# Relational pass of a graph network with FFN: epilogue and FFN of a node range as two chains, one range apart, spread over the gathers

## The chip, the cores and the metric

The kernel runs on one core of a Trainium2 chip. The metric is the device time of one execution in microseconds (us), as the median of several. The engines are TensorE (PE in the profile, its weight loads PEld), VectorE (DVE), ScalarE (ACT), GpSimd (POOL) and SyncE (SP). SP and POOL issue the DMAs of the part that is looked at here: SP plain loads and stores, POOL gathers of rows by a list of indices.

## The reference, cut to what matters

The input is a graph of 12,500 nodes with 256 features and 212,500 edges, which are sorted by their destination. Two layers follow one another, each a graph part and an FFN part. The change lies in the first layer:

```
x = x + L0_gnn(layernorm(x))        # per edge: weight * (x[src] @ block-diagonal W[relation]), summed at dst
x = x + L0_ffn(layernorm(x))        # rows picked by a router (top-k): gelu(xn @ w1 + b1) @ w2 + b2, times the router's weight
x = x + L1_gnn(layernorm(x))        # attention over the same edges
x = x + L1_ffn(layernorm(x))        # two of eight experts per row
```

The FFN of the first layer has 1024 hidden columns. This kernel computes it for all nodes, and weighs or drops it later, when the router's choice among all nodes is known.

## The kernel before, in words

The kernel has these stages, with their place in the profile. From 0 to 465 us it computes a table T0 in device memory: for each of 8 relations the products of all normalized nodes with that relation's block-diagonal matrix. From 465 to 2906 us runs the **relational pass** (`even_depths`). Its last chains end at 2979 us. Then come the choice of the router (`choose`, to 3055 us), the combination of FFN and nodes (to 3230 us), the attention pass over the same edges (to 6030 us) and the experts (to 7439 us).

In the relational pass the edges are cut into NT = 1661 tiles of 128. Tile t takes these steps:

- `fetch(t)`: POOL gathers 128 rows of 1 KB from T0 into one of 16 row buffers (L234, `row<-T,rowC`).
- `matrices(j)`: for 6 tiles at a time (SUB) DVE makes matrices `S`, 128 edges by 96 destinations (WIN): one where the edge goes to the destination (L922), times the edge's weight (L1017). There are 4 such buffers.
- `use(t)`: TensorE multiplies the gathered rows with `S` and adds the products in PSUM to the sums of the node range (L913, `bin<-S,row`). A range has 512 nodes (BIN), its sums lie transposed in two banks, and two ranges fit into the pool `psA`. There are 24 ranges of four node tiles and a last one of two. A range has some 68 edge tiles (1661 / 24.4).

The order of the work is written by hand with a small planner, `Plan`: a heap of pieces of work by step. A step is a tile of edges. `fetch(t)` is at step t, `use(t)` at step t + 3, `matrices(j)` at t - 8 of its first tile. The heap is run from its smallest step up, and what it emits fixes the order of instructions on PE, DVE, ACT and SP. POOL has the gathers alone.

When the last tile of a range has been added, the generator `summed(b, sums)` is put in a queue (`plan.queue(line, ...)`). A generator does a piece of work, yields a number of steps, and is continued that many steps later. The queue `line` runs one range's chain after another. Before the change one chain does all for a range, in 59 or 60 steps:

1. The node tiles are loaded (SP), the sums are copied from PSUM (`aT`, L962 on ACT, L963 on DVE).
2. For each of the four node tiles TensorE transposes the sums back (L195, `pt<-ident,aT`), and three steps later DVE adds them to the nodes (L970, `X<-xg,pt`).
3. DVE computes mean and variance of the rows (L201 to L215).
4. For each node tile DVE normalizes (L219, `xn`), one step later TensorE transposes (L195, `pt<-ident,xn`), DVE forms the router's weight (L983) and adds `xn` to `X` (L985), and two steps later the transposed rows are copied to `xT` (L189 on ACT or L191 on DVE, by turns).
5. FFN1: for each of 8 blocks of hidden columns two matmuls (L993, `ph<-xT,w1s`) and gelu on ACT (L995, `hT`), then two steps of distance.
6. FFN2: for each node tile 8 matmuls (L1001, `pt<-w2s,hT`) in two blocks of four, one step apart, then DVE adds b2 (L1007, `y`), and SP stores Y.

So within a range's 68 steps the epilogue (1 to 4) takes the first 31 or so, the FFN the next 28, and the last are free of both. A matmul in this program's 32-bit type leaves two records in the profile. PSUM has eight banks here: four for `psA`, two for `psh` (FFN1), two for `pst`, which the transposes and FFN2 share.

Of the kernel before, what the change touches and what calls it, by code (L numbers as in the profile page):

```python
# [23 lines left out]
F32 = mybir.dt.float32  # L24
# [9 lines left out]
PSUM = bass.MemoryType.PSUM  # L34

P = 128
# [10 lines left out]
SUB = 6  # L47
# [53 lines left out]
def gnn_ffn_kernel(ctx: ExitStack, tc: tile.TileContext, x, src, dst, etype, eweight, w_rel, wr, br,  # L101
                   fw1, fb1, fw2, fb2, W, att_src, att_dst, bias, Wg, bg, W1, b1, W2, b2, out):
    nc = tc.nc
    N, D = x.shape
# [23 lines left out]
    def rows(m):  # L128
        return P if m < NM - 1 else TAIL
# [55 lines left out]
    def evac(dst_ap, src_ap):  # L185

        evac_n[0] += 1
        if evac_n[0] % 2:
            nc.scalar.activation(dst_ap, src_ap, AF.Copy)  # L189
        else:  # L190
            nc.vector.tensor_copy(dst_ap, src_ap)  # L191

    def transpose(o, i):
        k = i.shape[0]
        nc.tensor.transpose(o, i, ident[:k, :k])  # L195
# [14 lines left out]
    def ln_stats(xg, mv, pool):  # L210

        st = pool.tile([P, 4, 6], F32, name="ln_st")
        for i in range(mv.shape[1]):
            nc.vector.bn_stats(st[:, i, :], xg[:, i, :])
            nc.vector.bn_aggr(mv[:, i, :], st[:, i, :])  # L215
        rstd_(mv, pool)

    def normalized(o, xr, mv):
        nc.vector.tensor_scalar(o, xr, mv[:, 0:1], mv[:, 1:2], op0=OP.subtract, op1=OP.mult)  # L219

    def load_nodes(tile_ap, table, ms, eng):

        full = [m for m in ms if rows(m) == P]
        if len(full) < len(ms):
            nc.gpsimd.memset(tile_ap[:, len(full), :], 0.0)
            m = ms[-1]
            eng.dma_start(tile_ap[:TAIL, len(full), :], table[m * P:m * P + TAIL, :])
        if full:
            m = full[0]
            eng.dma_start(tile_ap[:, :len(full), :],  # L230
                          table[m * P:(m + len(full)) * P, :].rearrange("(g p) d -> p g d", p=P))
# [205 lines left out]
    with ExitStack() as ta:  # L437
# [4 lines left out]
        pst = ta.enter_context(tc.tile_pool(name="ta_pt", bufs=2, space=PSUM))  # L442
# [4 lines left out]
        for b in range(NB):  # L447
            k, bl = divmod(b, NB // 2)
            nc.sync.dma_start(BD[bl * SB:(bl + 1) * SB, k, :, bl * SB:(bl + 1) * SB], w4[b])
        T0n = T0.rearrange("(n r) d -> n (r d)", r=R)  # L450
        for ms in GROUPS:
            G = len(ms)
# [4 lines left out]
            for i, m in enumerate(ms):  # L457
                xn = xp_.tile([P, D], F32, name="xn")
                normalized(xn, xg[:, i, :], mv[:, i, :])
                pt = pst.tile([P, 2, P], F32, name="pt")  # L460
                for k in range(2):
                    transpose(pt[:, k, :], xn[:, k * P:(k + 1) * P])
                xT = xp_.tile([P, 2, P], F32, name="xT")
# [11 lines left out]
    KH = FH // P  # L475
# [460 lines left out]
    def even_depths(AD, lcC):  # L936


        with ExitStack() as md:
# [8 lines left out]
            with ExitStack() as r1:  # L948
                wk = r1.enter_context(tc.tile_pool(name="r1_w", bufs=1))
                rw = r1.enter_context(tc.tile_pool(name="r1_r", bufs=16))  # L950
                psA = r1.enter_context(tc.tile_pool(name="r1_pa", bufs=2, space=PSUM))
                psh = r1.enter_context(tc.tile_pool(name="r1_ph", bufs=2, space=PSUM))
                pst = r1.enter_context(tc.tile_pool(name="r1_pt", bufs=2, space=PSUM))
                plan, line = Plan(), []

                def summed(b, sums):
                    ms = [m for m in range(b * BIN // P, (b + 1) * BIN // P) if m < NM]
                    G = len(ms)
                    xg = wk.tile([P, 4, D], F32, name="xg")
                    load_nodes(xg, x, ms, nc.sync)  # L960
                    aT = wk.tile([P, 2, BIN], F32, name="aT")
                    nc.scalar.activation(aT[:, 0, :G * P], sums[0][:, :G * P], AF.Copy)  # L962
                    nc.vector.tensor_copy(aT[:, 1, :G * P], sums[1][:, :G * P])  # L963
                    yield 3
                    for i, m in enumerate(ms):
                        pt = pst.tile([P, 2, P], F32, name="pt")
                        for k in range(2):
                            transpose(pt[:, k, :], aT[:, k, i * P:(i + 1) * P])
                        yield 3
                        nc.vector.tensor_tensor(X[:, m, :], xg[:, i, :], pt.rearrange("p k j -> p (k j)"), op=OP.add)  # L970
                    mv = wk.tile([P, 4, 2], F32, name="mv")
                    ln_stats(X[:, ms[0]:ms[0] + G, :], mv[:, :G], wk)
                    yield 1
                    xT = wk.tile([P, 2, 4 * P], F32, name="xT")
                    for i, m in enumerate(ms):
                        xn = wk.tile([P, D], F32, name="xn", bufs=2)
                        normalized(xn, X[:, m, :], mv[:, i, :])
                        yield 1
                        pt = pst.tile([P, 2, P], F32, name="pt")
                        for k in range(2):  # L980
                            transpose(pt[:, k, :], xn[:, k * P:(k + 1) * P])
                        junk = wk.tile([P, D], F32, name="junk")
                        nc.vector.scalar_tensor_tensor(junk, xn, 1.0, wrB, op0=OP.mult, op1=OP.mult,  # L983
                                                       accum_out=WT[:, m:m + 1])
                        nc.vector.tensor_tensor(X[:, m, :], X[:, m, :], xn, op=OP.add)  # L985
                        yield 2
                        evac(xT[:, :, i * P:(i + 1) * P], pt)
                    yield 2
                    hT = wk.tile([P, KH, 4 * P], F32, name="hT")
                    for f in range(KH):  # L990
                        ph = psh.tile([P, 4 * P], F32, name="ph")
                        for k in range(2):
                            nc.tensor.matmul(ph[:, :G * P], w1s[:, k, f * P:(f + 1) * P], xT[:, k, :G * P],  # L993
                                             start=k == 0, stop=k == 1)
                        nc.scalar.activation(hT[:, f, :G * P], ph[:, :G * P], AF.Gelu_apprx_tanh, bias=b1s[:, f:f + 1])  # L995
                        yield 2
                    yield 1
                    for i, m in enumerate(ms):
                        py = pst.tile([P, D], F32, name="pt")
                        for f in range(KH):  # L1000
                            nc.tensor.matmul(py, hT[:, f, i * P:(i + 1) * P], w2s[:, f, :],  # L1001
                                             start=f == 0, stop=f == KH - 1)
                            if f % 4 == 3:
                                yield 1
                        yield 1
                        y = wk.tile([P, D], F32, name="y", bufs=2)
                        nc.vector.tensor_tensor(y, py, b2B, op=OP.add)  # L1007
                        n = rows(m)
                        nc.sync.dma_start(Y[m * P:m * P + n, :], y[:n])

                add = windows(psA, lambda b, sums: plan.queue(line, plan.now + 1, summed(b, sums)))
                rows_, S_ = {}, {}

                def matrices(j):
                    n = min(SUB, NT - j * SUB)
                    S = one_hot(wk, lcC, j * SUB, n, bufs=4)
                    nc.vector.tensor_tensor(S[:, :n], S[:, :n],  # L1017
                                            ewC[:, j * SUB:j * SUB + n, None].to_broadcast([P, n, WIN]), op=OP.mult)
                    S_[j] = S

                def fetch(t):
                    rows_[t] = rw.tile([P, D], F32, name="row")
                    gather(rows_[t], T0, rowC[:, t:t + 1])

                def use(t):
                    g = rows_.pop(t)
                    add(t, lambda k: g[:, k * P:(k + 1) * P], S_[t // SUB][:, t % SUB, :])

                for t in range(NT):
                    if t % SUB == 0:  # L1030
                        plan.put(t - 8, lambda j=t // SUB: matrices(j))
                    plan.put(t, lambda t=t: fetch(t))
                    plan.put(t + 3, lambda t=t: use(t))
                with tc.manual_schedule(engines=ORDERED):
                    plan.run()
                nc.vector.tensor_scalar(WT, WT, brB, None, op0=OP.add)
            choose(WT)

            with ExitStack() as cb:
                wk = cb.enter_context(tc.tile_pool(name="cb_w", bufs=3))  # L1040
                pst = cb.enter_context(tc.tile_pool(name="cb_pt", bufs=4, space=PSUM))
                psy = cb.enter_context(tc.tile_pool(name="cb_py", bufs=4, space=PSUM))
                for ms in GROUPS:
                    G = len(ms)
# [8 lines left out]
                    for i, m in enumerate(ms):  # L1053
                        n = rows(m)
                        nc.sync.dma_start(X2[m * P:m * P + n, :], X[:n, m, :])
                        xn = wk.tile([P, D], F32, name="xn")
                        normalized(xn, X[:, m, :], mv[:, i, :])
                        pt = pst.tile([P, 2, P], F32, name="pt")
# [621 lines left out]
```

## Time and profile before

| what | value |
|---|---|
| median of 3 executions | 6972.26 us (6971.64 to 6975.37) |
| profiled execution | 7440.8 us, its span 7439.0 us |
| mean TensorE clock in it | 0.719 of full speed |
| relational gathers: first, last start | 464.9 us, 2905.9 us |
| PE, PEld, DVE, ACT, POOL busy over the span | 74%, 62%, 39%, 10%, 55% |

The profiled execution is 6.7% longer than the median. Times of single instructions come from it. A row of the groups reads: line, engine, operation, names of output and inputs, shapes, how often; then busy time in us and the mean ns of one; then the idle time ahead of these instructions and what ended most of it. "issue" is a wait for nothing that the profile shows. The wait's view reads: engine and line that wait, what they wait for, then us in total, times, and the longest.

### The profile page before, as it was taken

The page shows a single profiled execution, that of the slowest core. Times are in us where ns is not written, and L with a number is a line of the kernel's source. Part 1 is how long each engine was busy: PE and PEld are TensorE (multiplying, and loading weights), DVE is VectorE, ACT ScalarE, POOL GpSimd, SP SyncE. Part 2 cuts the span into 40 slices and gives each one's busy share as a digit, 9 for nine tenths or more (in the row PEclk, how much of TensorE's full clock was granted, in tenths as well). Part 3 has the DMA queues.
Part 4 walks back from the last instruction along what each step waited for, and adds up shares of the span by engine and source line. Part 5 has one row for each costly group of instructions (what it writes and reads, how often), then busy time and mean ns, then how long its engine had stood idle before and what let it go on. Part 6 is the DMA issues. An engine that isn't in the chain of part 4 may idle for free. (4 is left out here: it accounts for less than half of the span.)

```text
span 7439.0 us, 75728 instructions
## 1 busy us (share of the span) xinstructions
PE 5498.0 (74%) x26987; PEld 4635.6 (62%) x26987; DVE 2928.5 (39%) x7669; ACT 745.9 (10%) x1537; POOL 4095.7 (55%) x3768
## 2 busy tenths in 40 slices
PE   7967888887788887537777776767867775777775
PEld 3446667666677766427666676766766764666654
DVE  6633222323332222745556565565554650111110
ACT  2310000000000000110000000000000001112111
POOL 0036666666666664047777777777777742222222
PEclk9977787877778888765555555565555557888887
DMA  7753333333333332444444444444444425555555
GB/s 253 300 202 96 102 100 101 100 98 100 101 101 102 102 101 68 150 133 119 123 120 120 124 121 122 124 119 121 122 121 116 126 77 173 138 137 142 137 136 158
DMA packets 437371, 949.39 MB, mean 128 GB/s; under 512 B 84371, under 2 KB 293222, under 8 KB 410783
## 3 DMA queue, kind: packets, MB, share of 16 engines
q0 software_dynamic: 199872, 494.39, 25.6%
q1 hardware_dynamic: 237108, 450.03, 19.4%
q8 instruction: 217, 3.56, 0.2%
q14 instruction: 174, 1.42, 0.1%
HBM read 617.71 MB, written 228.88 MB: 114 GB/s over the span
## 5 line engine op out<-in xcount | busy, mean ns | idle before, releaser
L234 POOL DMA_INDIRECT rows<-T1A,srcC x1661 | 1867.0, 1124 | 684.0 <-issue 455.5
L234 POOL DMA_INDIRECT row<-T,rowC x1661 | 1655.5, 997 | 847.8 <-issue 327.2
L913 PE MATMUL bin<-S,rows 128*128 128x96 f32 (+5 forms) x7700 | 1724.1, 391 | 340.5 <-issue 235.6
L913 PEld LDWEIGHTS bin<-S,rows 128*128 128x128 f32 x7700 | 1604.1, 304 | 444.5 <-issue 315.6
L913 PEld LDWEIGHTS bin<-S,row 128*128 128x128 f32 x7700 | 1232.5, 241 | 237.4 <-issue 221.1
L913 PE MATMUL bin<-S,row 128*128 128x96 f32 (+5 forms) x7700 | 1248.7, 322 | 98.9 <-issue 94.0
L882 POOL DMA_INDIRECT O<-y,toI x210 | 326.7, 1556 | 907.0 <-DVE y L881 419.1
L872 PE MATMUL ph<-xT,we 128*128 128x256 f32 x1680 | 469.7, 442 | 267.7 <-DVE xT L191 262.8
L922 DVE TENSOR_TENSOR S<-lcC,col 128x576 f32<-128x576 f32 x554 | 415.9, 751 | 440.8 <-PE bin L913 175.8
L872 PEld LDWEIGHTS ph<-xT,we 128*128 128x128 f32 x1680 | 372.7, 227 | 344.0 <-DVE xT L191 275.6
L993 PE MATMUL ph<-xT,w1s 128*128 128x512 f32 (+1 forms) x800 | 426.1, 663 | 132.9 <-ACT hT L995 68.6
L1253 DVE TENSOR_TENSOR rows<-rows,w 128x1536 f32<-128x1536 f32 x277 | 484.8, 1750 | 79.6 <-issue 60.9
L861 DVE CAST toI<-xs 128x2 int32<-128x2 f32 x105 | 17.7, 169 | 1024.6 <-DMA O<-y,toI 820.9
L878 PE MATMUL py<-we,hT 128*128 128x256 f32 x1680 | 381.1, 379 | 5.7 <-DVE y L881 5.7
L1001 PE MATMUL pt<-w2s,hT 128*128 128x256 f32 x1568 | 378.5, 385 | 3.2 <-issue 3.1
L469 PE MATMUL pm<-BD,xT 128*128 128x512 f32 x784 | 351.1, 601 | 12.8 <-ACT xT L189 12.3
L878 PEld LDWEIGHTS py<-we,hT 128*128 128x128 f32 x1680 | 318.8, 190 | 50.9 <-DVE y L881 7.7
L195 PE MATMUL pt<-ident,xn 128*128 128x128 f32 x588 | 121.7, 317 | 289.1 <-DVE xn L219 176.0
L993 PEld LDWEIGHTS ph<-xT,w1s 128*128 128x128 f32 x800 | 153.9, 213 | 254.6 <-issue 180.4
L1001 PEld LDWEIGHTS pt<-w2s,hT 128*128 128x128 f32 x1568 | 284.7, 191 | 36.1 <-issue 4.5
L189 ACT ACTIVATE xT<-pt 128x256 f32<-128x256 f32 x301 | 115.2, 383 | 1840.2 <-PE pt L195 979.6
L195 PEld LDWEIGHTS pt<-ident,xn 128*128 128x128 f32 x588 | 79.9, 164 | 342.1 <-issue 317.2
(267 smaller groups left out, 4893.5 us busy)
## 6 DMA issues: line engine op xcount, KB each, us to landing
we<-Wall SPq DMA_DIRECT2D x105, 1026.0 KB
T<-tb SPq DMA_DIRECT2D x97, 1024.0 KB
dmB<-DMN SPq DMA_DIRECT2D x277, 192.0 KB
xs<-XS SPq DMA_DIRECT2D x105, 257.0 KB
row<-T,rowC POOLq DMA_INDIRECT x1661
rows<-T1A,srcC POOLq DMA_INDIRECT x1661
xg<-in_x_dram SPq DMA_DIRECT2D x48, 512.0 KB
T1A<-t SPq DMA_DIRECT2D x97, 130.0 KB
```

Of the source, the lines that this page charges most:

```text
L189: nc.scalar.activation(dst_ap, src_ap, AF.Copy)
L195: nc.tensor.transpose(o, i, ident[:k, :k])
L234: return nc.gpsimd.indirect_dma_start(out=o, out_offset=None, in_=table, in_offset=bass.IndirectOffsetOnAxis(ap=idx, axis=0))
L469: nc.tensor.matmul(pm, xT[:, k, :], BD[:, k, r4:r4 + 4, :], start=True, stop=True)
L872: nc.tensor.matmul(ph, we[:, k * EH + f * P:k * EH + (f + 1) * P], xT[:, k, :], start=k == 0, stop=k == 1)
L878: nc.tensor.matmul(py, hT[:, f, i * P:(i + 1) * P], we[:, A1 + f * D:A1 + (f + 1) * D], start=f == 0, stop=f == KE - 1)
L882: nc.gpsimd.indirect_dma_start(out=O2, out_offset=bass.IndirectOffsetOnAxis(ap=toI[:, i:i + 1], axis=0), in_=y, in_offset=None, compute_op ...
L913: nc.tensor.matmul(open_[b][k][:, lo - b * BIN:hi - b * BIN], lhs(k), S[:, lo - base:hi - base], start=False, stop=last[b] == t)
L922: nc.vector.tensor_tensor(S[:, :n], lcC[:, t:t + n, None].to_broadcast([P, n, WIN]), col[:, None, :WIN].to_broadcast([P, n, WIN]), op=OP.i ...
L993: nc.tensor.matmul(ph[:, :G * P], w1s[:, k, f * P:(f + 1) * P], xT[:, k, :G * P], start=k == 0, stop=k == 1)
L1001: nc.tensor.matmul(py, hT[:, f, i * P:(i + 1) * P], w2s[:, f, :], start=f == 0, stop=f == KH - 1)
L1253: nc.vector.tensor_tensor(r, r, group[g]["w"][:, o:o + c, :, None].to_broadcast([P, c, H, CH]), op=OP.mult)
```

## The change

The change cuts the chain of a range in two and gives the second part its own queue, `lineF`.

- `summed(b, sums)` keeps the epilogue (1 to 4), with longer distances: 5 steps after the copies, 2 between transposes and add, 2 after each add, 2 after the statistics, 5 between normalizing and transposing, 1 after the copy to `xT`. It takes 55 steps. At its end it queues `depths(ms, xT)` on `lineF`, three steps later.
- `depths` is the FFN (5 and 6). A single FFN1 matmul is followed by a distance of 2 or 1 steps, gelu by 1; FFN2's matmuls stand one step apart each. It takes 65 steps, and so runs beside the epilogue of the range after it.
- `xT` gets two buffers, `xn` one. The pool `pst` has one bank, and FFN2 has one of its own (`psy`, `py`).
- `matrices(j)` is put at t - 4 instead of t - 8.

```diff
-                pst = r1.enter_context(tc.tile_pool(name="r1_pt", bufs=2, space=PSUM))
-                plan, line = Plan(), []
+                pst = r1.enter_context(tc.tile_pool(name="r1_pt", bufs=1, space=PSUM))
+                psy = r1.enter_context(tc.tile_pool(name="r1_py", bufs=1, space=PSUM))
+                plan, line, lineF = Plan(), [], []
...
-                    yield 3
+                    yield 5
                     for i, m in enumerate(ms):
                         pt = pst.tile([P, 2, P], F32, name="pt")
                         for k in range(2):
                             transpose(pt[:, k, :], aT[:, k, i * P:(i + 1) * P])
-                        yield 3
+                        yield 2
                         nc.vector.tensor_tensor(X[:, m, :], xg[:, i, :], pt.rearrange("p k j -> p (k j)"), op=OP.add)
+                        yield 2
                     mv = wk.tile([P, 4, 2], F32, name="mv")
                     ln_stats(X[:, ms[0]:ms[0] + G, :], mv[:, :G], wk)
-                    yield 1
-                    xT = wk.tile([P, 2, 4 * P], F32, name="xT")
+                    yield 2
+                    xT = wk.tile([P, 2, 4 * P], F32, name="xT", bufs=2)
                     for i, m in enumerate(ms):
-                        xn = wk.tile([P, D], F32, name="xn", bufs=2)
+                        xn = wk.tile([P, D], F32, name="xn")
                         normalized(xn, X[:, m, :], mv[:, i, :])
-                        yield 1
+                        yield 5
...
                         evac(xT[:, :, i * P:(i + 1) * P], pt)
-                    yield 2
+                        yield 1
+                    plan.queue(lineF, plan.now + 3, depths(ms, xT))
+
+                def depths(ms, xT):
+
+                    G = len(ms)
                     hT = wk.tile([P, KH, 4 * P], F32, name="hT")
                     for f in range(KH):
                         ph = psh.tile([P, 4 * P], F32, name="ph")
                         for k in range(2):
                             nc.tensor.matmul(ph[:, :G * P], w1s[:, k, f * P:(f + 1) * P], xT[:, k, :G * P],
                                              start=k == 0, stop=k == 1)
+                            yield 2 - k
                         nc.scalar.activation(hT[:, f, :G * P], ph[:, :G * P], AF.Gelu_apprx_tanh, bias=b1s[:, f:f + 1])
-                        yield 2
+                        yield 1
                     yield 1
                     for i, m in enumerate(ms):
-                        py = pst.tile([P, D], F32, name="pt")
+                        py = psy.tile([P, D], F32, name="py")
                         for f in range(KH):
                             nc.tensor.matmul(py, hT[:, f, i * P:(i + 1) * P], w2s[:, f, :],
                                              start=f == 0, stop=f == KH - 1)
-                            if f % 4 == 3:
+                            if f < KH - 1:
                                 yield 1
-                        yield 1
+                        yield 0
                         y = wk.tile([P, D], F32, name="y", bufs=2)
                         nc.vector.tensor_tensor(y, py, b2B, op=OP.add)
...
+                        yield 1
...
-                        plan.put(t - 8, lambda j=t // SUB: matrices(j))
+                        plan.put(t - 4, lambda j=t // SUB: matrices(j))
```

## The prediction

> **What bounds the kernel now.** I read the page's busy lines and slices first, to find the stage, then the costliest groups, then the groups, waits and windows of this stage alone (460 to 2950 us). The page's groups give the two loops of gathers:
>
> ```profile
> L234 POOL DMA_INDIRECT rows<-T1A,srcC x1661 | 1867.0, 1124 | 684.0 <-issue 455.5
> L234 POOL DMA_INDIRECT row<-T,rowC x1661 | 1655.5, 997 | 847.8 <-issue 327.2
> ```
>
> The second row is the stage that the change touches: 1661 gathers, busy 997 ns each. The first row is the later attention pass, which is left alone. The stage's gathers by tile, with what ended POOL's idle time, and below it the same view of 490:566, the first range, in which no epilogue or FFN is running yet:
>
> ```profile
> L234 POOL DMA_INDIRECT row<-T,rowC x1661: 947/953/1557, 464.9 to 2905.9; - x185
> ...
>   issue: 327.2, 1045
>   PE bin L913: 265.9, 382
>   remote: 172.6, 90
> ...
> L234 POOL DMA_INDIRECT row<-T,rowC x53: 947/953/1457, 491.1 to 564.8; - x53
> ```
>
> Numbers to take: the pace is (2905.9 - 464.9) / 1660 = 1.471 us per gather; POOL is ready again 327.2 / 1045 = 0.313 us after a gather if nothing holds it, so an unheld gather takes 0.997 + 0.313 = 1.310 us. The rest, 0.161 us per gather, is waiting: a gather writes one of 16 row buffers and waits for the matmuls (L913) that read that buffer 16 gathers earlier. In the first range, without any epilogue or FFN, the pace is (564.8 - 491.1) / 52 = 1.417: most of the wait is there before TensorE has anything but bins to do.
>
> By stretches (us from:to, length; then busy PE, PEld, DVE, ACT, POOL, each with its count; PEclk, DMA share, GB/s):
>
> ```profile
> 460.00:560.00 100.00, 53.45 (x244) 47.58 (x245) 19.97 (x33) 0.00 (x0) 64.00 (x65) 0.55 0.43 136
> 1500.00:1600.00 100.00, 82.19 (x429) 69.99 (x429) 28.77 (x68) 6.86 (x11) 68.54 (x69) 0.79 0.35 100
> 2500.00:2600.00 100.00, 81.30 (x435) 68.19 (x435) 29.33 (x69) 6.86 (x11) 67.98 (x69) 0.79 0.35 100
> ...
> 1512.00:1516.00 4.00, 0.96 (x6) 0.75 (x6) 3.52 (x18) 0.00 (x0) 3.08 (x4) 0.50 0.35 103
> 1516.00:1520.00 4.00, 4.00 (x20) 4.00 (x21) 2.99 (x9) 0.00 (x0) 3.09 (x4) 0.50 0.33 93
> ...
> 1560.00:1564.00 4.00, 4.00 (x23) 3.10 (x23) 0.00 (x0) 0.69 (x1) 3.00 (x4) 1.00 0.32 98
> 1588.00:1592.00 4.00, 4.00 (x21) 4.00 (x21) 0.00 (x0) 0.00 (x0) 2.31 (x3) 0.50 0.30 87
> ```
>
> No engine is full: TensorE 82%, POOL 68%. A range (68 gathers, 100 us) repeats: an epilogue where TensorE runs at half clock and waits for DVE (1512:1516), an FFN where it is full and at full clock (1560:1564), then bins alone at half clock (1588:1592), catching up.
>
> **What the Trainium skill says.** "TensorE: Matmul & The Clock Gate", Part 1: the array runs at half clock after an idle window of about 3.4 us and at full clock after a busy one. The trace agrees: windows of 4 us stand at 0.50 or 1.00, and dense FFN windows are those at 1.00. "SBUF — State Buffer", Who interferes with whom: a DVE operation with two SBUF inputs contends with GpSimd's reads. Agrees in kind: gathers take 953 ns in the median and up to 1557; the mean excess of 44 ns is not altered by moving DVE work about. "Perfetto Trace Analysis", Per-instruction lifecycle: a matmul's end in a profile is an estimate, so I take no matmul's release of a buffer from its recorded end.
>
> **The change, part by part.** By kind and count nothing is added or removed: 1661 gathers, 7700 + 800 + 1568 records of L913, L993 and L1001, the same gelus, adds, node loads and Y stores. Only order and buffers change.
>
> (1) *Spreading.* TensorE's need per range at full clock: bins 4.64 records per gather at 0.107 us (the distance of starts in full-clock windows) x 68 = 34 us; FFN1 32 x 0.43 = 13.8; FFN2 64 x 0.22 = 14; transposes 16 x 0.2 = 3. Sum 65 us of 100, before and after. Before, the 28 us of FFN lie in some 27 of 68 steps, where with the bins they need 28 + 27 x 0.50 = 41 us against 27 x 1.47 = 40 us that the gathers give: TensorE falls behind there, and more so when it enters late and at half clock. After, an FFN matmul stands alone between the bins of every gather: 0.96 us per step against 1.47. The lag goes and with it the load's part of the waits. Its size: the load-free pace of the first range, 1.417, as the bound that a spread load can reach if waits at light load stay: (1.471 - 1.417) x 1593 gathers = 86 us. The other bound: all waits go, (1.471 - 1.310) x 1593 = 256 us. The lower bound is 0: the waits of the first range show that light load alone does not remove them. I take 86: after the change TensorE has 0.96 us of work per step at full clock, and in the first range it has the bins at half clock, 4.64 x 0.213 = 0.99, so the two are alike in what they ask per gather.
>
> (2) *Longer distances in the epilogue.* TensorE now waits for DVE in front of the transposes, with all bins behind it:
>
> ```profile
> PE pt L195 <- DVE xn L219: 126.9, 22, 13.7
> PE pt L195 <- DVE mv L208: 73.4, 12, 9.2
> PE ph L993 <- ACT hT L995: 68.6, 23, 6.8
> POOL row L234 <- PE pt L1001: 42.6, 51, 2.4
> ```
>
> 200.3 us over 24 ranges is 8.3 us per range; 5 steps (7 us) instead of 1 between normalizing and transposing, and 7 steps behind the statistics (4 x (0.40 + 0.18) of L214 and L215 and some 11 small operations at 0.17, about 4.2 us of DVE) cover it. Gelu's 68.6 us are covered by 4 steps between pairs instead of 2. None of these is a gain of its own: the gathers see them through (1). The one-hot matrices (two DVE operations of about 0.75 us, L922 and L1017, for 6 gathers) are issued 4 steps ahead instead of 8. They are still 7 steps, some 10 us, ahead of their use, and a DVE clump (statistics plus one pair) is about 6 us: 0. Their buffer is free 12 steps after its last use instead of 8, so the 175.4 us that L922 waited for L913 shrink: DVE is no bound, 0.
>
> (3) *New waits.* The FFN output has one bank instead of sharing two: the next node tile's first matmul waits for the add to y (0.42 us) and the hand-over, about 0.75 us, four times a range, bins queued behind it. The transposes' bank is single too: the add or evacuation is due 2 or 3 steps (3 to 4 us) before the next transpose. Worth 3 us per range if DVE is free; with DVE in a statistics clump up to 5 us each, 20 us. TensorE has 100 - 65 = 35 us to spare: 0 is taken, bounds 0 to the rival below. SP's queue holds node loads and Y stores only; a range's Y stores now come beside the next range's epilogue, in front of the following node load by some 13 steps: 0. POOL's queue holds gathers alone, in the old order: 0.
>
> (4) *The end.* From the last gather to the top-k is 2979 - 2906 = 73 us: the rest of range 23's epilogue, its FFN (28 us), range 24's epilogue and FFN one after another. After, FFN2 of range 22 (14 us) is still to come as well, then FFN of 23 (28) and of 24 (14), but the epilogues lie beside them: 56 us, plus 10 waits of 0.75 for y and a start, 64 to 85. Taken +5 (bounds -9 to +12).
>
> **Sum.** -86 + 5 = -81 us of the profiled execution (7440.8, span 7439.0). That execution is 6.7% above the median of 6972.26, and no view says where; scaled by 6972.26 / 7440.8 = 0.937 it is -76: 6896 us.
>
> **The rivals.** *All waits go* (chance 0.22): if the first range's waits come from its half clock, an even load, which keeps the clock up, removes them: -256 x 0.937 + 5 = -235, 6737 us. For it: the FFN windows at 1.00 and POOL's wait for L913 being the chief one. Against it: 1.417 without load. *Gathers set the pace already* (0.17): POOL's excess is not TensorE's load, or only the profiled execution has it; 0 and the end's few us: 6972. For it: the pace hardly differs between 53% and 82% of TensorE. *A new wait in the old one's place* (slower, 0.1): TensorE and DVE hand single banks to and fro, 4 + 8 times a range. It decides when these waits pass TensorE's spare 35 us, 2.9 us each; at 3.2 us it is (38.4 - 35) x 24 = +82: 7054. Against it: the handed work takes 0.42 us and has steps of its own. To slower I add 0.08 for an end worse than +12 or a pace that is the same or a little worse with it (6985 to 7000). A drop of the clock is part of this: evenly spread matmuls at half clock need 1.93 us per step, but it takes over 69% of the stage at half clock (0.963 / (1 - 0.69 / 2) = 1.47), where now it is 42%. That the order isn't as described is excluded: the order of instructions shows single FFN matmuls between 2 to 4 bin records over the whole range.
>
> **How the numbers follow.** Likeliest (0.43): -86 with half to one and a half of its size, 6850 to 6935. With "all waits go" faster comes to 0.65; same, within 0.2% (14 us, what a measurement of this kernel can tell from no change), 0.17; slower 0.18. The range from 6725 to 6995 leaves out about 0.1 at each side or less.
>
> **What would show it.** Right: the gathers' pace near 1.42 from the second range on, PEclk steady near 1.0 in 4-us windows instead of 0.50 and 1.00 by turns, the wait of L195 for xn and mv near zero, POOL's wait for L913 below 265.9, and about 75 us between the last gather and the top-k. Wrong: a pace of 1.47 (the gathers bound) or 1.31 (all waits), PEclk near 0.5, or long waits of the FFN2 matmul for y or of transposes for the adds.

## The result: 0.4% slower, where 1.1% faster was forecast

In a comparison of 16 executions each the kernel after takes 7005.4 us (6983.6 to 7027.9), the kernel before 6975.0 us (6954.3 to 6997.9). The ratio is 1.004, with a 95% interval from 1.0026 to 1.0054: the change costs some 30 us. A second comparison on another occasion gave 7008.2 against 6979.6, ratio 1.0045 (1.0029 to 1.0061).

One thing has to be known to read the numbers: executions of the kernel before stand at one of two levels, near 6975 us or near 7450 us, and all executions of one series are at the same level; the profiled execution of before, on which the prediction rests, is at the upper one, the profile of after at the lower.

The profile of after has a span of 7007.5 us. Its two loops of gathers, from the page's groups:

```profile
L234 POOL DMA_INDIRECT rows<-T1A,srcC x1661 | 1885.8, 1135 | 512.2 <-issue 438.6
L234 POOL DMA_INDIRECT row<-T,rowC x1661 | 1660.4, 1000 | 578.0 <-issue 217.9
```

The attention pass, whose code is unchanged, has 512 us of idle time on POOL, where the first profile had 684. The two profiles are thus not at the same level. The relational gathers by tile, after:

```profile
L234 POOL DMA_INDIRECT row<-T,rowC x1661: 948/953/2090, 466.0 to 2642.3; - x185
...
  issue: 217.9, 715
  PE bin L913: 216.6, 675
  remote: 61.5, 2
```

The pace is (2642.3 - 466.0) / 1660 = 1.311 us, which is the pace that the prediction had worked out for gathers that nobody holds up (1.310). PE bin ends 675 of the waits, but 216.6 / 675 = 0.321 us: nearly all are the plain distance between two gathers.

What does before look like at the same level? There is no profile of the whole kernel before there, but there are two that stand for it: that of the kernel before with 19 row buffers instead of 16, whose time is that of before (ratio 0.9997, 0.9985 to 1.0008), and that of the kernel before cut off behind the first layer, with its 16 buffers. In this order:

```profile
L234 POOL DMA_INDIRECT row<-T,rowC x1661: 949/953/1552, 465.7 to 2640.6; - x185
```

```profile
L234 POOL DMA_INDIRECT row<-T,rowC x1661: 942/946/1542, 467.3 to 2628.4; - x185
```

The pace is (2640.6 - 465.7) / 1660 = 1.310 and (2628.4 - 467.3) / 1660 = 1.302. The first range, from which the prediction had taken 1.417 as the pace without load, stands at 1.312 and 1.308. So before had no wait left for the change to remove. The waits of the two kernels in this stage, before with 19 buffers first, then after (who waits for whom, us in total, times, longest):

```profile
POOL row L234 <- issue: 267.0, 876, 0.3
POOL row L234 <- PE bin L913: 159.4, 523, 0.3
PE pt L195 <- DVE xn L219: 0.2, 1, 0.2
```

```profile
POOL row L234 <- issue: 217.9, 715, 0.3
POOL row L234 <- PE bin L913: 216.3, 674, 2.6
PEld py L1010 <- DVE y L1016: 12.3, 48, 0.3
```

The last column is what to read: no gather of before waits more than 0.3 us, which is its distance to the one ahead. After the change the longest wait is 2.6 us. Summed over what goes beyond 0.305 us (the median distance in the traces), gathers wait 0.2 us in the first and 11.1 us, 13 gathers, in the second. The wait of L195 for `xn`, 126.9 us in the first profile, is 0.2 us in before at this level.

The end. These are the first instruction of the router's choice, in before with 19 buffers and in after:

```profile
L546 DVE COPY key<-WT x1: 211/211/211, 2706.2 to 2706.2; 128x98 f32<-128x98 f32 x1
```

```profile
L546 DVE COPY key<-WT x1: 213/213/213, 2718.9 to 2718.9; 128x98 f32<-128x98 f32 x1
```

From the last gather's start that is 2706.2 - 2640.6 = 65.6 us before and 2718.9 - 2642.3 = 76.6 us after: 11 us longer. In the two kernels the last bins (L913) and FFN2 records are, by line from 2640 us on, before first:

```profile
L913 PE MATMUL bin<-S,row x16: 421/421/529, 2639.6 to 2645.0; 128*128 128x96 f32 x16
L1001 PE MATMUL pt<-w2s,hT x96: 379/379/380, 2662.9 to 2703.6; 128*128 128x256 f32 x96
```

```profile
L913 PE MATMUL bin<-S,row x56: 246/275/275, 2641.8 to 2653.6; 128*128 128x96 f32 x56
L1010 PE MATMUL py<-w2s,hT x160: 379/379/484, 2653.7 to 2716.2; 128*128 128x256 f32 x160
```

Before, the last bin starts 4.4 us after the last gather starts, after the change 11.3 us: TensorE trails. And 160 FFN2 records instead of 96 are still to come, those of range 22 among them (17 us). Against these 24 us stands the serial epilogue of range 24, some 10 us with TensorE idle for 7 of them, which now lies beside the FFN of 23. This and a few smaller distances leave 11 us.

The clock. Two stretches of 100 us of after, then stretches of 4 us of it (the columns are those of the prediction's table):

```profile
1500.00:1600.00 100.00, 93.64 (x488) 75.07 (x487) 32.84 (x79) 6.86 (x11) 76.00 (x77) 0.81 0.39 113
2500.00:2600.00 100.00, 85.89 (x484) 60.35 (x484) 34.19 (x80) 6.75 (x11) 76.83 (x77) 1.00 0.41 116
1540.00:1544.00 4.00, 4.00 (x16) 3.48 (x17) 0.00 (x0) 0.00 (x0) 3.08 (x4) 0.50 0.35 108
1556.00:1560.00 4.00, 4.00 (x14) 2.97 (x15) 0.00 (x0) 0.00 (x0) 3.09 (x4) 0.50 0.38 104
1572.00:1576.00 4.00, 4.00 (x24) 2.93 (x23) 0.42 (x1) 0.69 (x1) 3.09 (x4) 1.00 0.35 98
```

TensorE is without a gap at 1540 and at 1556 and yet at half clock. In most ranges it stays so for 27 to 38 us, from the end of one FFN2 well into the next FFN1. These stretches have a place in the range. The last 11 of a range's 68 tiles have edges in the next range too: such a tile leaves 8 bin records instead of 4, each with fewer than 96 columns. After the change 10 FFN1 records stand among the bins of these 11 tiles. Two such places of after, the 11 tiles each time:

```profile
1533.00:1561.80 28.80, 28.80 (x104) 22.65 (x103) 0.89 (x2) 1.97 (x3) 21.91 (x23) 0.50 0.36 106
2514.60:2529.50 14.90, 14.90 (x103) 12.00 (x101) 0.36 (x1) 2.16 (x4) 11.24 (x13) 1.00 0.46 138
```

At full clock TensorE needs 14.9 / 11 = 1.35 us per tile there, about what the gathers give; at half clock 28.8 / 11 = 2.6, and it falls behind. In after 22 of 23 such places take 26 us or more, in its second profile 18, in that of the short version 16; in before with 19 buffers, where FFN2's end stands among these tiles, none takes more than 17. All 13 gathers that wait come 26 to 30 tiles behind the first of the 11, and so wait for a row buffer that these tiles, or the four behind them, still hold. What brings the clock down and what lifts it is not shown. In after each half-clock stretch sets in behind 3.4 us in which TensorE was busy for 2.9 us or less; in before with 19 buffers the clock falls at this place in every range, for 10 to 14 us, behind 3.4 us without a gap.

Over 565:2600 the mean clock is 0.82 after, and 0.79 in before with 19 buffers:

```profile
565.00:2600.00 2035.00, 1908.71 (x9740) 1500.79 (x9739) 666.56 (x1573) 152.33 (x246) 1551.04 (x1553) 0.82 0.39 112
```

### The profile page after: what moved, and what is told of

Read it like the earlier page. It is cut to its first block, busy times and chain, and to the rows that moved or that the text cites. A ratio compares the mean times of both kernels' runs of the same rounds, so it can differ in the third digit from the quotient of the medians.

```text
span 7007.5 us, 75678 instructions
## 1 busy us (share of the span) xinstructions
PE 5626.2 (80%) x26987; PEld 4626.3 (66%) x26987; DVE 2921.9 (42%) x7669; ACT 745.9 (11%) x1537; POOL 4118.2 (59%) x3768
## 5 line engine op out<-in xcount | busy, mean ns | idle before, releaser
L913 PE MATMUL bin<-S,rows 128*128 128x96 f32 (+5 forms) x7700 | 1738.2, 400 | 246.3 <-DVE rows L1263 244.7
L913 PEld LDWEIGHTS bin<-S,rows 128*128 128x128 f32 x7700 | 1624.2, 312 | 345.9 <-DVE rows L1263 265.9
L913 PEld LDWEIGHTS bin<-S,row 128*128 128x128 f32 x7700 | 1296.7, 238 | 554.5 <-issue 261.0
L913 PE MATMUL bin<-S,row 128*128 128x96 f32 (+5 forms) x7700 | 1342.6, 319 | 135.2 <-DMA row<-T,rowC 123.8
L882 POOL DMA_INDIRECT O<-y,toI x210 | 326.8, 1556 | 910.6 <-DVE y L881 409.3
L1001 PE MATMUL ph<-xT,w1s 128*128 128x512 f32 (+1 forms) x800 | 538.5, 767 | 0.0
L1010 PE MATMUL py<-w2s,hT 128*128 128x256 f32 x1568 | 479.7, 394 | 8.1 <-DVE y L1016 3.6
L922 DVE TENSOR_TENSOR S<-lcC,col 128x576 f32<-128x576 f32 x554 | 414.8, 749 | 46.2 <-PE bin L913 45.9
L469 PE MATMUL pm<-BD,xT 128*128 128x512 f32 x784 | 351.1, 601 | 12.8 <-ACT xT L189 12.3
L1213 DVE TENSOR_TENSOR al<-al,rows 128x20 f32<-128x20 f32 (+1 forms) x332 | 53.1, 176 | 670.8 <-DMA rows<-T1A,srcC 643.5
L965 DVE COPY aT<-bin 128x512 f32<-128x512 f32 (+1 forms) x25 | 17.0, 680 | 646.8 <-PE bin L913 389.0
L1004 ACT ACTIVATE hT<-ph,b1s 128x512 f32<-128x512 f32 (+1 forms) x200 | 135.7, 679 | 1354.5 <-PE ph L1001 1354.5
L469 PEld LDWEIGHTS pm<-BD,xT 128*128 128x128 f32 x784 | 145.6, 191 | 189.6 <-issue 154.2
```

Source lines behind the costliest of these rows:

```text
L469: nc.tensor.matmul(pm, xT[:, k, :], BD[:, k, r4:r4 + 4, :], start=True, stop=True)
L882: nc.gpsimd.indirect_dma_start(out=O2, out_offset=bass.IndirectOffsetOnAxis(ap=toI[:, i:i + 1], axis=0), in_=y, in_offset=None, compute_op ...
L913: nc.tensor.matmul(open_[b][k][:, lo - b * BIN:hi - b * BIN], lhs(k), S[:, lo - base:hi - base], start=False, stop=last[b] == t)
L922: nc.vector.tensor_tensor(S[:, :n], lcC[:, t:t + n, None].to_broadcast([P, n, WIN]), col[:, None, :WIN].to_broadcast([P, n, WIN]), op=OP.i ...
```

## The experiments

Each series of kernels ran beside the kernel before on the same chip. The first series (up to the FFN chain at the old distances) was at the upper level, the others at the lower.

**A copy of before.**

> The kernel before, unchanged, for a second profile: the first one is 466 us longer than the timed runs, the one of after is not (7009 against 7005). Ratio 1.000. Theory A (POOL alone sets the pace in the timed runs of both kernels, and a gather takes longer on the mean after the change because more of them meet a DVE operation): if the profile comes out near 6975 us, the gathers' pace is about 1.295 us and the end from the last gather to the top-k about 73 us, against 1.311 and 77 after. Theory B (the pace is the same, the end is longer by the FFN2 of one more range): pace 1.31 and an end of about 50 us. If the profile is near 7440 again, the waits for L913 belong to the profiled execution of this order of work.

Measured: 7451.0 us against 7452.6, ratio 1.0003 (0.999 to 1.0015). Its profile repeats the first one:

```profile
L234 POOL DMA_INDIRECT row<-T,rowC x1661: 948/957/1541, 466.6 to 2910.7; - x185
...
  PE bin L913: 244.5, 394
```

The long profile is thus no doing of the profiler: timed executions without it stand at 7450 too. The preparation ends at the same 466 us at both levels; in the trace 95 in 100 gathers land their rows within 3.3 us of their issue, and half within 2.44, at both. What differs is what the trace has of the semaphores. In before with 19 buffers each of the 2495 increments of TensorE's semaphore in the relational pass lies within 60 ns of a matmul's recorded end; in the first profile 551 of 2251 do, and the median distance is 362 ns instead of 14. In the preparation it is 15 ns at both levels. As the prediction recalls, a matmul's recorded end is an estimate, so the trace can't say whether the increments are late or the matmuls longer than recorded. It also lacks records at the upper level: 6929 of the gathers' 26,576 increments are there, where the other has 26,525. The level doesn't go by the chip: one chip number stands at 7450 in this series and at 6981 in that of the short kernels. What makes the difference is open.

**The matrices at t - 4, alone, in before.**

```diff
-                        plan.put(t - 8, lambda j=t // SUB: matrices(j))
+                        plan.put(t - 4, lambda j=t // SUB: matrices(j))
```

> Before, with the one-hot matrices at t - 4 instead of t - 8, nothing else. Theory A: their DVE operations meet other gathers; between -10 and +30 us. Theory B: 6975 us, ratio 1.000.

Measured, upper level: 7443.9 us against 7452.6, ratio 0.9984 (0.9973 to 0.9995). This part alone costs nothing there; if anything, it gains a little.

**After, with the matrices back at t - 8.** The same edit the other way.

> After, with the one-hot matrices back at t - 8. Theory A: back by part of the 30 us if the place of these operations is what counts (6975 to 7005). Theory B: 7005, unchanged against after.

Measured, upper level: 7511.0 us against 7452.6 of before, ratio 1.0074 (1.0053 to 1.0094). After itself was only met at the lower level, so what this edit does to after stays open. But the profile shows what the other parts do at the upper level:

```profile
L234 POOL DMA_INDIRECT row<-T,rowC x1661: 948/957/1541, 465.6 to 2967.3; - x185
...
  PE bin L913: 335.0, 429
```

```profile
PEld py L1010 <- DVE y L1016: 141.0, 40, 10.5
```

The pace is 1.507, where before has 1.471 at this level. FFN2's weight load waits 141 us for the add to `y`, up to 10.5 us at a time, where it is 12.3 us at the lower level. That this hand-over of the single bank is what slows the pace isn't shown; POOL's waits for L913 grew as well, from 265.9 to 335.0. Spreading did not take waits away there either.

**After, with the FFN chain at the old distances.**

```diff
                                              start=k == 0, stop=k == 1)
-                            yield 2 - k
                         nc.scalar.activation(hT[:, f, :G * P], ph[:, :G * P], AF.Gelu_apprx_tanh, bias=b1s[:, f:f + 1])
-                        yield 1
+                        yield 2
...
-                            if f < KH - 1:
+                            if f % 4 == 3:
                                 yield 1
-                        yield 0
+                        yield 1
```

> After, with the FFN chain on its own queue but with the old distances (two FFN1 matmuls together, two steps per gelu; FFN2 in blocks of four), so that an FFN takes 29 steps and not 65. Theory A: DVE's work is as in after but for the adds to y, so 6995 to 7010. Theory B: the FFN2 of range 22 is done before the last gather, so the end is 14 us shorter: about 6990. If TensorE's even load were itself what costs, 6975.

Measured, upper level: 7527.1 us, ratio 1.0091 (1.0069 to 1.0113). The numbers expected were for the lower level; it tells only that a dense FFN with one bank is no remedy at the upper level.

**After, unchanged.**

> The kernel after, unchanged, beside the kernel before on the same chip: executions of before take 6975 us on one chip and 7452 on another, with the difference in the two gather loops. Theory A (where a chip's TensorE reports its work late, single banks and spread matmuls make TensorE and DVE wait for each other more often): ratio 1.005 to 1.010 at the level of 7450, the pace of the gathers near 1.50; 1.004 at the level of 6975. Theory B (the cost is the end alone): 1.001 to 1.002 at the level of 7450.

Measured: the lower level, 7008.2 us against 6979.6, ratio 1.0045 (1.0029 to 1.0061). From the last gather's start to L546 it is 2723.2 - 2646.0 = 77.2 us, and 18 gathers wait, 10.7 us in all. The first result stands, and so does the longer end. After unchanged was not met at the upper level, so the larger ratio expected there stays untested.

**Before with 19 row buffers.**

```diff
-                rw = r1.enter_context(tc.tile_pool(name="r1_r", bufs=16))
+                rw = r1.enter_context(tc.tile_pool(name="r1_r", bufs=19))
```

> Before, with 19 row buffers instead of 16. If gathers wait because TensorE is late by some tiles and catches up: at the level of 7450 the pace falls from 1.471 by 0.03 to 0.06, 50 to 100 us less. If TensorE is short of throughput there: no change. At the level of 6975 (POOL at its own pace): no change.

Measured, lower level: 6978.6 us against 6979.6, ratio 0.9997 (0.9985 to 1.0008), as expected for POOL at its own pace. Its profile was shown above.

**After with the old distances in the epilogue.**

```diff
-                    yield 5
+                    yield 3
...
-                        yield 2
+                        yield 3
                         nc.vector.tensor_tensor(X[:, m, :], xg[:, i, :], pt.rearrange("p k j -> p (k j)"), op=OP.add)
-                        yield 2
...
-                    yield 2
+                    yield 1
...
-                        yield 5
+                        yield 1
...
-                        yield 1
+                    yield 2
```

> After, with the old distances in the epilogue (3, 3, 0, 1, 1, 2 steps), the FFN chain as in after. Theory A: the hand-overs between TensorE and DVE lie closer, so slower than after by 0 to 40 us. If the longer distances themselves put DVE's operations in the way of the gathers: faster than after by 10 to 30 us.

Measured: 6983.9 us against 6979.6 of before, ratio 1.0002 (0.999 to 1.0015). The 24 us below after are all of the loss but what the comparison can't tell. The profile has no gather that waits (0.2 us in all beyond 0.305), an end of 2698.4 - 2639.2 = 59.2 us, and nearly the clock that the prediction had expected of the whole change:

```profile
565.00:2600.00 2035.00, 1770.25 (x9766) 1351.86 (x9766) 677.72 (x1576) 157.69 (x252) 1561.32 (x1555) 0.93 0.39 113
```

A clock of 0.93 instead of 0.79, with TensorE's busy time 159 us less than in before with 19 buffers, and no time gained: TensorE doesn't set the pace. Only 7 of the 23 places with tiles of two ranges take 26 us or so here, and no gather waits behind them. The reason that I had expected (DVE's operations less in the way of the gathers) isn't it: gathers take 1.005 us in the mean here and 1.000 in after.

**After with the last three FFNs at the old distances.**

```diff
+                    late = ms[0] >= 22 * 4
...
-                            yield 2 - k
+                            yield 0 if late and k == 0 else 2 - k
...
-                            if f < KH - 1:
+                            if f < KH - 1 and (not late or f == 3):
```

> After, with the FFN of the last three ranges (22 to 24) at the old distances, so that the FFN2 of range 22 is done before the last gather. The tail from the last gather to the top-k falls from 77 us to about 62. Theory B: 12 to 15 us less than after, half of the loss at the level of 6975. If the end is not the cause: within 5 us of after.

Measured: 7006.8 us against 6979.6, ratio 1.0036 (1.0022 to 1.005): no gain. The end did not shrink, it is 2738.9 - 2657.8 = 81.1 us. FFN2 of range 22 now stands ahead of the last bins in TensorE's order, but TensorE could not keep up with it: it runs until 17.5 us after the last gather's start, the last bin starts 21.0 us after it, and the last gathers waited up to 3.9 us each. The work that I had moved out of the end had only moved in front of the bins.

**Before, after, and after with the old distances in the epilogue, cut short.** Each lacks the attention pass and the experts; the output is filled with the nodes after the first layer.

```diff
             even_depths(AD, lcC)
-            filled = even_gat(AD, lcC)
-        slots(filled)
+        whole = N // 176 * 176
+        nc.sync.dma_start(out[:whole, :].rearrange("(a b) d -> a (b d)", a=176),
+                          X2[:whole, :].rearrange("(a b) d -> a (b d)", a=176))
+        if whole < N:
+            nc.sync.dma_start(out[whole:, :], X2[whole:N, :])
```

> Before, without the attention pass and the experts (the output is filled with the nodes as they stand after the first layer), so that only the preparation, the relational pass, the router's choice and the combination are timed. A base for the next two: about 2960 us where before takes 6975, about 3240 where it takes 7450.

> After, cut in the same way. If the loss lies in the relational pass and its end, as the profiles say (end +11, gathers +2 to +5): 14 to 30 us more than b_short. If a part of the 29 us lies in the attention pass or the experts, whose code is the same: 0 to 14 us more.

> After with the old distances in the epilogue, cut in the same way. By the profiles (end 59 us against 66 of before and 77 of after, gathers the same): 5 to 9 us less than b_short, 17 to 25 less than a_short. If its equality with before in the long form is the true measure: within 3 us of b_short.

Measured: 2979.9 us (2972.7 to 2981.5) before, 3001.7 (2994.9 to 3007.2) after, 2975.3 (2974.5 to 2978.1) with the old distances in the epilogue. The loss of after is 22 us here, so at least most of it lies in the relational pass and its end; the 7 us that lack to the 29 of the long kernels are within their spread. In the profiles of this pair the gathers wait 0.5 us (before) and 18.1 us (after, 25 waits) beyond 0.305, and the ends are 66.5 and 77.2 us: 18 + 11 = 29 in one execution each, against 22 in the median of five. The version with the old distances is 26.4 us below after, as its profile has it (an end of 59.2 us, 0.1 us of waits), but its 4.6 us below before are within the spread of the five.

**The FFN chain put later, with the old distances in the epilogue.**

```diff
-                    plan.queue(lineF, plan.now + 3, depths(ms, xT))
+                    plan.queue(lineF, plan.now + 27, depths(ms, xT))
```

> The kernel with after's FFN chain and the old distances in the epilogue, but the FFN chain put 27 steps instead of 3 behind the epilogue's end, so that it starts about where it does in after. If the loss comes from the FFN's late start (FFN2 of range 22 then stands behind the last gather): the end is back at about 75 us and the time near 7000, 15 to 25 us above the version without the delay. If it comes from the long distances in the epilogue themselves: the time stays near 6984.

Measured: 6982.3 us against 6981.9 of before, ratio 1.0007 (0.9993 to 1.0022). The FFN's late start lengthens the end from 59.2 to 2706.8 - 2639.0 = 67.8 us, less than the 75 expected, but no loss against before can be told, and gathers wait 0.9 us in all. The mean clock is 0.90. So what costs in after is the long distances in the epilogue, together with the late start that they bring, and not the late start alone. Which of the six distances it is, and why the clock is more often down with them, stays open; so does a part of the matrices at t - 4, which all versions of after at the lower level have.

**One DVE operation per tile for the matrices.** In before, and then with the old distances in after's epilogue:

```diff
-                    S = one_hot(wk, lcC, j * SUB, n, bufs=4)
-                    nc.vector.tensor_tensor(S[:, :n], S[:, :n],
-                                            ewC[:, j * SUB:j * SUB + n, None].to_broadcast([P, n, WIN]), op=OP.mult)
+                    S = wk.tile([P, SUB, WIN], F32, name="S", bufs=4)
+                    for i in range(n):
+                        t = j * SUB + i
+                        nc.vector.tensor_scalar(S[:, i, :], col[:, :WIN], lcC[:, t:t + 1], ewC[:, t:t + 1],
+                                                op0=OP.is_equal, op1=OP.mult)
```

> Before, with each one-hot matrix made by one DVE operation per tile (compare with the destination, times the edge's weight, both as scalars per partition) instead of a comparison and a product of two SBUF tensors for six tiles. In the profiles of this chip state the gathers beside the product (L1017) take about 0.27 us longer, 277 times: 75 us. If the second SBUF input is the reason: about 60 to 75 us faster than before, and hardly any gather over 1 us. If any DVE operation beside a gather slows it: no change or slower, as there are six operations for two. Where before takes 7450 us: half of it or less.

Measured: 6905.5 us against 6981.4, ratio 0.9897 (0.9882 to 0.9912): 76 us.

```profile
L234 POOL DMA_INDIRECT row<-T,rowC x1661: 949/953/1209, 466.2 to 2562.3; - x185
```

The pace is 1.263, the mean gather 0.958 instead of 1.005 us. POOL does set the time of this stage, and what had lengthened its gathers is DVE's pair of operations, not TensorE. DVE is not less busy with the matrices than before (429 us against 417), so a shorter DVE load isn't the reason.

> After's FFN chain, the old distances in the epilogue, and one DVE operation per tile for the one-hot matrices. By the measured parts (6905 for the matrices in the kernel before; end 6 us shorter): 6898 to 6908, ratio 0.989, with the gathers at 1.262 us. If TensorE, which now has 1.26 us per step, falls behind in its half-clock stretches: over 6915.

Measured: 6903.0 us against 6981.9, ratio 0.9891 (0.9869 to 0.9913), with a pace of 1.263. The number came as expected, but not its working. The end isn't 6 us shorter, as these lines show, the version without the change of order first:

```profile
L546 DVE COPY key<-WT x1: 213/213/213, 2628.3 to 2628.3; 128x98 f32<-128x98 f32 x1
```

```profile
L546 DVE COPY key<-WT x1: 211/211/211, 2632.0 to 2632.0; 128x98 f32<-128x98 f32 x1
```

It is 2628.3 - 2562.3 = 66.0 us without it and 2632.0 - 2562.5 = 69.5 with it: at this pace TensorE trails again, by 14.0 us behind the last gather's start instead of 4.6. The gain is that of the matrices, and the order adds nothing that can be told.

## Why the prediction was wrong, point by point

**The base of the sum.** The step that failed is the first: 0.161 us of waiting per gather was read from an execution at 7440.8 us and brought to the median by a factor, 0.937, as if the 468 us lay evenly over the kernel. They lie in the two loops of gathers: 2441 us of relational gathers against 2175 at the lower level, and in the attention pass 2797 against 2632, which is 431 of the 468. Where the kernel was timed, the 0.161 us were zero: 1.310 us per gather, with 0.2 us of waiting in all 1661. The rival "gathers set the pace already ... or only the profiled execution has it" named this mechanism at 0.17, but with no loss. The loss itself was priced only in the small part of "slower" with a larger end or a pace a little worse (0.08, 6985 to 7000): both came, and the result lies just beyond. The evidence was on the table: a gap of 6.7% whose place no view showed, and a pace of 1.417 without load.

**Spreading: -86 us.** Measured: 0 from less waiting, and 11 to 18 us of new waiting. The working took an even load and full clock for granted. The load isn't even: 4.64 bin records per gather is the mean of 57 tiles with 4 and 11 with 8, and the FFN1 matmuls now stand among the 11. The clock isn't full: in most ranges it is half at just this place, and TensorE needs 2.6 us per tile against 1.31 that come (the prediction's 1.93 is the mean over a range). It falls behind by more than the 16 row buffers allow, and a few gathers (13 to 25) wait up to 2.3 us longer each. The Trainium skill, "TensorE: Matmul & The Clock Gate", Part 1, names a busy window as what lifts the clock; here windows that the profile shows busy throughout did not (1540:1544, 1556:1560). The prediction's own table had such windows, 1516:1520 and 1588:1592, each busy for 4.00 of 4.00 us at 0.50: its "The trace agrees" held for the FFN windows alone. The rival of a dropping clock had its point of decision at 69% of the stage; about a third of the stage at half clock was enough, since it comes in one piece per range and at the heaviest tiles.

**Longer distances.** Right that the waits of L195 for `xn` and `mv` vanish, but at the level that was timed they did not exist before. The distances were costed at nothing, and they are what costs: with the old ones the loss is gone (ratio 1.0002).

**New waits.** Right at the lower level: 12.3 us of FFN2 waiting for `y` in 48 hand-overs, inside TensorE's spare time. The rival of hand-overs in place of the old wait is not what the gathers wait for there. At the upper level a wait of that kind is large (141 us), with a pace above that of before.

**The end: +5, bounds -9 to +12.** The mechanism was right, and 77 us after lay in the 64 to 85 given; the term was mis-sized by its base, 73 us from the upper level where 66 hold at the lower. Measured +11, with 7 us of TensorE's trailing bins that the sum did not have.

**The total.** In the traces of the short pair 11 us at the end and 18 of waits make 29, against 22 in the medians. In the long ones the same sum is 22, but of the 29 to 30 us measured only 12 to 16 show up to L546, as the gathers of before with 19 buffers happened to be 6 to 10 us longer in all. Single executions scatter too much to divide the loss more finely.

## What to carry to other kernels

If a profiled execution is several per cent longer than the timed ones, find out which stage holds the difference before a stall in it is priced: compare a stage whose code doesn't change. Ask first whether the engine that sets the pace has any idle time beyond its own distance between instructions; if not, no reordering of the others gains, and what a longer pipeline can still change is the end of the loop, where work is no longer covered, and new waits. And a load that is even in the mean can be uneven where it counts: look for the steps with more work than the others (here the tiles of two ranges), keep other work off them, and leave slack there for TensorE's half clock.

## What the hardware showed beyond that

A gather that starts while L922 or L1017 runs (each DVE, two inputs in SBUF, about 0.75 us) takes up to 1.55 us instead of 0.95, and the less the later in the operation it starts. These two make 79 of the 87 us by which the gathers of before with 19 buffers exceed 0.953 us each. The rest shows that it is the inputs and not just any DVE operation: beside L985 (two inputs in SBUF, 0.42 us) 21 gathers took 1.099 us in the mean, beside L1007 (one input in PSUM, 0.42 us) 27 gathers took 0.953. This fits an exclusive lock as the Trainium skill, "SBUF — State Buffer", Who interferes with whom, has it for such operations against GpSimd's reads. The form with one SBUF tensor took 76 us out of the time. The two levels, some 470 us apart and nearly all of it in the loops of gathers, were the other surprise; what selects them is open.
